# Four-layer graph network on one core: layer 0's attention queries, table building and a long convolution cut into steps and placed elsewhere

## The chip, the core and the metric

The kernel runs on one core of a Trainium2 chip. The core has a matrix engine (TensorE, PE in the profile; its weight loads are shown as PEld), a vector engine (VectorE, DVE), a scalar engine (ScalarE, ACT), a general engine (GpSimd, POOL) and an engine that issues transfers (SyncE, SP). Each takes its instructions in the order of its own queue. The transfers run on 16 DMA engines. The metric is the time on the device in microseconds (us), as the median of the runs; lower is better.

## What is computed

The input is a graph of 1250 nodes with 512 features and 21,250 edges (with 1250 loops in it, and 1250 more for GATv2's mean edges). Four layers follow one another. Each adds a graph network and a linear attention, both of the normalized input, and then a feed-forward part:

```python
xn = _layernorm(x)
x = x + _L0_gnn_ref(xn, ...) + _L0_mix_ref(xn[None], ...)[0]
x = x + _L0_ffn_ref(_layernorm(x)[None], ...)[0]
...                                        # layers 1, 2, 3 alike
```

Three of these twelve parts matter here. The attention of layer 0 and the graph network beside it, which is three GATv2 layers:

```python
# _L0_mix_ref: 8 heads of 64
q, k, v = split(xn @ W_qkv)                # each [1250, 512]
q_phi, k_phi = elu(q) + 1, elu(k) + 1
KV    = einsum('bhnd,bhne->bhde', k_phi, v)
denom = einsum('bhnd,bhd->bhn', q_phi, k_phi.sum(axis=2))[..., None] + 1e-6
out   = einsum('bhnd,bhde->bhne', q_phi, KV) / denom
return out @ W_out + b_out

# _L0_gnn_ref
for k in range(3):
    xl, xr = x @ Wl[k] + bl[k], x @ Wr[k] + br[k]
    m     = leaky_relu(xl[src2] + xr[dst2] + ea2 @ We[k])
    alpha = segment_softmax(m @ att[k], dst2)
    out   = segment_sum(xl[src2] * alpha[:, None], dst2) + b_out[k]
    x     = relu(layernorm(out + x) * gamma[k] + beta[k])
```

The graph network of layer 2 (EGC), where four aggregated bases are weighted for each of 8 heads:

```python
bases = x @ W_bases                                        # [1250, 4 * 64]
agg   = segment_sum(bases[src] * norm, dst).reshape(n, 4, 64)
w     = (x @ W_comb + b_comb).reshape(n, 8, 4)
out   = einsum('nhb,nbf->nhf', w, agg) + conv_bias + x @ W_res + b_res
return relu(layernorm(out) * gamma + beta)
```

And the feed-forward part of layer 2: a convolution over the nodes (3 taps, gelu, then 3 taps to 10 numbers) gives each node its two experts of ten; a shared convolution (9 taps to 256 channels, silu, then 1 tap) is added:

```python
logits = conv1d(gelu(conv1d(xt, rc_w1) + rc_b1), rc_w2) + rc_b2
vals, idx = top_k(logits, 2);  gates = softmax(vals)
y  = sum over the two experts e of gate * (elu(x @ e_w1[e] + e_b1[e]) @ e_w2[e] + e_b2[e])
sh = conv1d(silu(conv1d(xt, sh_w1) + sh_b1), sh_w2) + sh_b2
return layernorm(x + y + sh) * ln_g + ln_b
```

## The kernel before

The nodes stand in ten tiles of 128 rows (`NT`), the last with 98; x stays in SBUF. A product of a tile with a 512 x 512 matrix (`nat`, L171) is four matmuls, each of which appears in the profile as two passes, so eight rows. `evac` brings results out of PSUM by DVE (L136) and ACT (L134) in turn. `add_to_x` (L185) adds a tile to x on DVE. The order on the engines is that in which the program issues, unless a pool or a dependence holds an instruction back; on SP some stretches have an order written out by hand.

**The start of layer 0, `gat_first`.** The nodes are normalized, turned into `xnT` and stored in memory (`xtab`). For the first GATv2 layer, `gat_tables` builds two tables tile by tile, a left one (513 columns) and a right one, and stores them. Then the linear attention runs, first the keys and values (`P`, `ks`, folded with `W_out` into `kvo`), then the query tiles: for each of the ten tiles a product with `wq` (L171), relu and exp on ACT (L746, L747), five DVE operations (L748, L810, L812, L815, L817), four transposes, a product with `kvo` (L171) and an addition to x. All of this is a generator, of which one step is taken after each one-hot group of the edges (`onehot_steps`, L550 to L573). Then `mean_edges` forms the mean of the edges' features for the loops, by way of tables in memory (the gather L614), and the generator is emptied. When all tiles of this stage are free, the GATv2 layers begin.

**The GATv2 layers, `gatv2_fast` and `gat_layer`.** Edges are worked on in groups of four tiles of 128 (47 groups, 188 tiles). POOL gathers the left rows of a group's edges (`xl`, L231, nine buffers), SP loads the one-hot rows (`nb`, L1251, through ACT's L1267) and the right rows of a block (`hl`, L1244), PE multiplies them (`right`, L1280 and L1281), DVE adds and weights them (L1293, L1296), and later PE mixes them by the attention weights into a block of 107 nodes (`more`, L1347). Four groups make a block. When a block is done, it is normalized, and the tables of the next layer are built from it with the same `gat_tables` (L1166), as late work of the loop. The loop `for i in range(FT + 3)` issues a bit of every kind of work per tile; at its end, a loop empties what is left in the three queues `edge`, `todo` and `late`. The next layer's weights and vectors are prepared during a layer, in steps (`gat_weights`, with a POOL memset L1122 and an addition).

**Layer 2's EGC, `layer2_attn`.** For each of ten tiles: the residual product, the product of the one-hot counts with the bases (L2571, after a cast `cs` of 1280 columns), scalings by the degree (`ag`), and for each of four bases one DVE product of 128 x 512 (`m`, L2585) and one POOL addition (L2588). Beside it the linear attention of layer 2 is issued step by step.

**Layer 2's feed-forward, `layer2_ffn`.** Three forms of the transposed input (L2687, DVE) let a convolution with two neighbouring outputs use fewer products. A piece of the convolution's weights is three loads (L2623) and three POOL operations (L2624 to L2626). `conv` runs the products (L2649) for one half of the channels at a time. The order is: forms; router convolution with gelu (L2701); the shared convolution with silu (L2766), while the routing goes on; the ten second products (L2780, L2782); then the loop over 29 expert tiles (`experts`, L2316 to L2348), which loads the expert's weights (1 MB) and the tokens (`xe`, 256 KB) of a tile up to three tiles ahead.

Of the kernel before, what the change touches and what calls it, by code (L numbers as in the profile page):

```python
# [57 lines left out]
class Net:  # L58
# [675 lines left out]
    def linear_attention_steps(self, xn, xT, w_qkv, w_out, b_out, qscale, finish, added=None,  # L734
                               need=None):
# [14 lines left out]
        with self.tc.tile_pool(name="la", bufs=1) as p, \  # L750
# [6 lines left out]
            ks = p.tile([128, D], F32, name="ks")  # L757
            for half in range(2):
                if half:
                    wq = self.weight(w_qkv[:, 0:D], 4, D)  # L760
                    if qscale != 1.0:
                        nc.gpsimd.tensor_scalar(wq, wq, qscale, None, op0=ALU.mult)
# [23 lines left out]
            kvo = p.tile([128, HT, D], F32, tag="k", name="kvo")  # L786
# [13 lines left out]
            yield  # L800
            Q, QT = {}, {}
# [308 lines left out]
    def gat_weights(self, L, p):  # L1110
# [17 lines left out]
        hl = p.tile([128, 2, D], F32R, tag="tro", name="wehl")  # L1128
# [25 lines left out]
    def gat_tables(self, L, p, t, xT, bank):  # L1154
# [7 lines left out]
        def product(name, c):  # L1162
            def f():
                if c == 0:
                    d[name] = bank()
                nc.tensor.matmul(d[name], lhsT=xT(c), rhs=L[name][:, c, :], start=c == 0,  # L1166
                                 stop=c == 3)
                if c == 3:
                    (left if name == "wl" else right)(d[name])
            return f  # L1170

        def left(m):
            o = p.tile([128, D + 1], F32, tag="tlo", name="tlo")
            nc.scalar.copy(o[:, :D], m)
# [5 lines left out]
        def right(m):  # L1180
            o = p.tile([128, 2, D], F32R, tag="tro", name="tro")
            nc.scalar.copy(o[:, 0, :], m)
# [3 lines left out]
        return [product(name, c) for name in ("wl", "wr") for c in range(4)]  # L1186

    def gatv2_fast(self, L, xtab):
# [5 lines left out]
        with self.tc.tile_pool(name="gat", bufs=2) as p, self.weights(2, 1):  # L1194
            big = p.tile([128, 1], F32, name="big", bufs=1)
            nc.vector.memset(big, 2.0 * BIG)
            self.gat_linear(L, p, p)
            for k in range(3):
                otab = self.dram.tile([NP, D], F32, name="x%d" % (k + 1))
                L = self.gat_layer(L, p, xtab, otab, big)  # L1200
                xtab = otab

    def gat_layer(self, L, p, xtab, otab, big):
# [6 lines left out]
        def prepare():  # L1210
# [6 lines left out]
            if nxt is not None:  # L1217
                nxt.update(self.gat_vectors(k + 1, p))
                steps = self.gat_weights(nxt, p)
# [16 lines left out]
        def load(g):  # L1236
            xl = p.tile([128, GE, W], F32, tag="xl", name="xl", bufs=9)
# [117 lines left out]
        def finish(b):  # L1355
# [44 lines left out]
            def across():  # L1400
# [10 lines left out]
                for t in whole:  # L1411
                    for f in self.gat_tables(nxt, p, t, lambda c, t=t: X[t][:, c, :],
                                             lambda: self.bank("tab", [128, D])):
# [41 lines left out]
        for i in range(FT + 3):  # L1455
# [17 lines left out]
            if i < FT:  # L1473
                right(i)
            if 2 <= i < FT + 2:
# [13 lines left out]
        while edge or todo or late:  # L1489
# [6 lines left out]
            for _ in range(2):  # L1496
                if late:
                    late.popleft()[1]()
        return nxt

    def run(self, fast):
# [4 lines left out]
        with self.tc.tile_pool(name="arm", bufs=1) as self.arm:  # L1506
# [23 lines left out]
            with self.psum():  # L1530
# [36 lines left out]
    def gat_first(self, pv, xtab):  # L1567
        nc, I = self.nc, self.I
        L = self.gat_vectors(0, pv)
        with self.tc.tile_pool(name="l0", bufs=1) as p, \  # L1570
# [3 lines left out]
            with self.tc.tile_pool(name="edge", bufs=1, side="right") as pe, \  # L1574
# [7 lines left out]
                for t in range(NT):  # L1582
# [8 lines left out]
                    lambda o, d: nc.vector.tensor_scalar(o, d, 1e-6, None, op0=ALU.add))  # L1591
                next(attention)

                def steps():
                    for t in range(NT):
                        for i, f in enumerate(self.gat_tables(
# [3 lines left out]
                            if i % 4 == 3:  # L1600
                                yield
                    yield from attention
# [7 lines left out]
                for _ in steps:  # L1610
                    pass
# [699 lines left out]
    def experts(self, table, n, rowI, act):  # L2311
# [5 lines left out]
        with self.tc.tile_pool(name="ex", bufs=2) as p, \  # L2317
                self.tc.manual_schedule(engines={mybir.EngineType.SP}):
            def load(i):
                xe = p.tile([128, D], F32, tag="xe", name="xe", bufs=4)  # L2320
                nc.sync.dma_start(xe, self.rin[i * 128:(i + 1) * 128, :])
                row = nc.sync.value_load(rowI[0:1, i:i + 1], min_val=0, max_val=(n - 1) * 128)
                w = p.tile([128, 2050], F32, tag="w", name="w", bufs=4)
                nc.sync.dma_start(w, table[bass.ds(row, 128), :])
                return xe, w

            ahead = [load(i) for i in range(3)]
            for i in range(ntiles):
                xe, w = ahead.pop(0)
                if i + 3 < ntiles:  # L2330
                    ahead.append(load(i + 3))
# [16 lines left out]
                nc.scalar.dma_start(self.rout[i * 128:(i + 1) * 128, :], o)  # L2348

# [134 lines left out]
    def layer2_attn(self):  # L2484
        nc, I = self.nc, self.I
        added = self.both_added()
        with self.tc.tile_pool(name="l2", bufs=1) as p:
# [17 lines left out]
            with self.tc.tile_pool(name="egc", bufs=2) as tmp, \  # L2505
# [55 lines left out]
                for t in range(NT):  # L2561
# [5 lines left out]
                    self.evac(cs, ct)  # L2567
                    go()
                    y = self.mm([128, parts * 256])
                    for s in range(NT):  # L2570
# [6 lines left out]
                    nc.vector.tensor_scalar(af, y[:, :256], dinv[:, t:t + 1], None,  # L2577
                                            op0=ALU.mult)
# [4 lines left out]
                    for b in range(4):  # L2583
                        m = tmp.tile([128, 8, 64], F32, tag="m", name="m")
                        nc.vector.tensor_tensor(  # L2585
                            m, wt[:, :, b:b + 1].to_broadcast([128, 8, 64]),
                            ag[:, b:b + 1, :].to_broadcast([128, 8, 64]), op=ALU.mult)
# [11 lines left out]

    def layer2_ffn(self):  # L2600
        nc, I = self.nc, self.I
        keep = self.begin_tail("l2t")
        with self.tc.tile_pool(name="l2f", bufs=1) as p, ExitStack() as right:
# [5 lines left out]
            with ExitStack() as es:  # L2609
# [5 lines left out]
                G = {}  # L2615

                def piece(src, f, j):

                    g = cp.tile([128, 4, 4, 128], F32, tag="cw", name="cw", bufs=5)
                    g1 = cp.tile([128, 4, 128], F32, tag="g1", name="g1")  # L2620
                    for i, dst in ((0, g[:, 0]), (2, g[:, 3]), (1, g1)):
                        k = 4 * (3 * j + i)
                        nc.sync.dma_start(dst, src[f][:, k:k + 4, :])  # L2623
                    nc.gpsimd.tensor_tensor(g[:, 1], g[:, 0], g[:, 3], op=ALU.add)  # L2624
                    nc.gpsimd.tensor_tensor(g[:, 2], g[:, 1], g1, op=ALU.subtract)
                    nc.gpsimd.tensor_tensor(g[:, 1], g[:, 1], g1, op=ALU.add)  # L2626
                    G[src.tensor.name, f, j] = g

                rc1, sh1 = I["L2_ffn_rc_w1p"], I["L2_ffn_sh_w1p"]
                order = [(rc1, f, 0) for f in range(4)] + [(sh1, f, j) for f in range(2)  # L2630
# [541 lines left out]
```

## Time and profile before

| | us |
|---|---|
| runs | 4534.72, 4537.75, 4541.73 |
| median | 4537.75 |
| profiled execution | 4585.94 |
| its span, first to last instruction | 4584.0 |

The profiled execution is one of its own, so times read from it are compared with its 4585.94 and not with the median. Where its span goes, by the stages of the program:

| stage | from | to |
|---|---|---|
| layer 0: start, tables, attention, one-hots | 18 | 312 |
| gathers of GATv2 layer 0 | 312.7 | 685.9 |
| gathers of GATv2 layer 1 | 770.9 | 1133.3 |
| gathers of GATv2 layer 2 | 1214.9 | 1572.4 |
| layer 0's feed-forward | 1622 | 1890 |
| layer 1: attention and graph network; feed-forward | 1890; 2880 | 2880; 3101 |
| layer 2: EGC and attention; feed-forward | 3101; 3397 | 3397; 3811 |
| layer 3: attention and graph network; feed-forward | 3811; 4226 | 4226; 4584 |

Between the gathers of two GATv2 layers lie some 80 to 85 us in which the last blocks of the one are finished, the last tables built, and the first groups of the next one fetched.

A row of the timeline or of the groups of instructions gives the line, the engine, the operation, out<-in, the shapes and how often it ran; what stands behind the bar or in square brackets is the idle time of the engine just before, and what ended it. A row of the busy time by stretch gives the stretch, its length, and for each engine its busy time and number of instructions; then the clock that PE was granted as a share of the full one, the mean share of the DMA engines in use, and GB/s.

### The profile page before, as it was taken

The numbers are of one execution on the slowest core, as the hardware profiler recorded it, in microseconds if no ns is written. First come the engines' busy times: TensorE is split into PE (matmuls) and PEld (weight loads), VectorE is DVE, ScalarE is ACT, GpSimd is POOL, SyncE is SP. The second block draws the span as 40 slices with busy tenths as digits, with TensorE's granted clock in tenths as the row PEclk, the third lists the DMA queues.
The fourth block names the chain that finished last, engine by engine and source line by source line (L and its number), as shares of the span: only waits on it lengthen the run. The fifth ranks groups of instructions, "written<-read, shape, count | busy, mean of one in ns | idle before, by whom it ended". The sixth has DMA issues, their size and how long they took to land. (4 is left out here: it accounts for less than half of the span.)

```text
span 4584.0 us, 49281 instructions
## 1 busy us (share of the span) xinstructions
PE 3946.8 (86%) x15451; PEld 2434.6 (53%) x15466; DVE 2706.4 (59%) x6387; ACT 1502.9 (33%) x2738; POOL 1402.3 (31%) x1339
## 2 busy tenths in 40 slices
PE   6988998899788866799999999997969975898796
PEld 3435554555354444444788876564546552454474
DVE  5358784878398865533796767314692136587301
ACT  2213332334133354110364446122221122455121
POOL 2027662766366501102000000103253003676101
PEclk9989998999899978899999999999989997997798
DMA  6446664666466423401421110392012185565695
GB/s 221 150 123 199 184 188 138 192 185 187 130 180 189 145 66 105 121 18 59 147 68 42 44 41 21 140 336 80 12 54 71 69 282 154 162 205 170 244 338 188
DMA packets 283000, 647.57 MB, mean 141 GB/s; under 512 B 61673, under 2 KB 108905, under 8 KB 267322
## 3 DMA queue, kind: packets, MB, share of 16 engines
q1 hardware_dynamic: 169290, 357.13, 23.5%
q0 software_dynamic: 73088, 234.75, 17.9%
q10 hardware_dynamic: 40352, 52.44, 3.4%
q8 instruction: 127, 2.08, 0.2%
q14 instruction: 143, 1.17, 0.1%
HBM read 528.87 MB, written 120.65 MB: 142 GB/s over the span
## 5 line engine op out<-in xcount | busy, mean ns | idle before, releaser
L231 POOL DMA_INDIRECT xl<-xl,srcI x564 | 606.6, 1075 | 309.4 <-issue 137.4
L1347 PE MATMUL more<-xl,wT 128*128 128x512 f32 x1128 | 578.5, 600 | 26.8 <-ACT wT L1337 25.3
L1280 PE MATMUL mm<-hl,oh 121*128 121x512 f32 x564 | 419.6, 744 | 89.7 <-DVE s L1293 29.7
L1293 DVE TENSOR_TENSOR s<-xl,mm 128x512 f32<-128x512 f32 x534 | 355.0, 680 | 99.9 <-PE mm L1281 42.3
L1296 DVE SCALAR_TENSOR_TENSOR junk<-s,att 128x512 f32<-128x512 f32 x534 | 409.8, 767 | 6.2
L2099 PE MATMUL more<-hh,e 128*128 128x259 f32 x1600 | 384.0, 386 | 11.1 <-ACT o L2042 8.9
L2099 PEld LDWEIGHTS more<-hh,e 128*128 128x128 f32 x1600 | 295.0, 191 | 75.6 <-issue 16.0
L171 PE MATMUL mm<-w,xnT 128*128 128x512 f32 x640 | 307.7, 620 | 13.7 <-DVE xnT L136 5.3
L231 POOL DMA_INDIRECT g<-routed_out,getI x60 | 64.7, 1079 | 676.7 <-DMA routed_out<-o 490.0
L231 POOL DMA_INDIRECT hs<-gcn_h,srcI x188 | 215.5, 1146 | 96.5 <-issue 35.9
L1347 PEld LDWEIGHTS more<-xl,wT 128*128 128x128 f32 x1128 | 196.5, 192 | 86.2 <-ACT wT L1337 34.4
L1281 PE MATMUL mm<-hl,oh 121*128 121x512 f32 x564 | 238.2, 422 | 0.0
L1280 PEld LDWEIGHTS mm<-hl,oh 121*128 121x128 f32 x564 | 111.6, 198 | 232.6 <-issue 135.0
L2649 PE MATMUL mm<-form,cw 128*128 128x312 f32 (+1 forms) x640 | 181.2, 445 | 23.9 <-POOL cw L2626 10.5
L171 PEld LDWEIGHTS mm<-w,xnT 128*128 128x128 f32 x640 | 123.8, 198 | 141.6 <-issue 125.2
L2019 ACT ACTIVATE e<-r,hh 128x512 f32<-128x512 f32 (+1 forms) x240 | 154.2, 646 | 132.5 <-PE more L2099 121.5
L1267 ACT ACTIVATE oh<-nb 112x512 fp32r<-112x512 bf16 x141 | 88.5, 629 | 327.4 <-DMA nb<-nbt 232.9
L2925 PE MATMUL more<-hl,oh 128*128 128x512 f32 x376 | 166.3, 545 | 31.0 <-ACT hl L2885 11.2
L1166 PE MATMUL tab<-w,xT 128*128 128x512 f32 x320 | 165.1, 614 | 19.9 <-DVE junk L1176 18.1
L2022 ACT ACTIVATE e<-r,a 128x512 f32<-128x512 f32 (+1 forms) x240 | 152.3, 646 | 69.4 <-DVE e L2024 57.2
L2024 DVE TENSOR_TENSOR e<-e,e 128x512 f32<-128x512 f32 (+1 forms) x240 | 142.0, 598 | 51.5 <-ACT e L2019 45.1
L1281 PEld LDWEIGHTS mm<-hl,oh 121*128 121x128 f32 x564 | 113.1, 201 | 106.9 <-issue 105.4
(623 smaller groups left out, 7748.6 us busy)
## 6 DMA issues: line engine op xcount, KB each, us to landing
w<-L_ffn_Wp SPq DMA_DIRECT2D x64, 1024.0 KB
w<-L_ffn_table SPq DMA_DIRECT2D x56, 1025.0 KB
neg<-ntab SPq DMA_DIRECT2D x80, 320.0 KB
nb<-nbt SPq DMA_DIRECT2D x141, 128.0 KB
hl<-xr SPq DMA_DIRECT2D x36, 448.0 KB
xr<-tro SPq DMA_DIRECT2D x30, 512.0 KB
xe<-routed_in SPq DMA_DIRECT2D x56, 256.0 KB
routed_out<-o ACTq DMA_DIRECT2D x56, 256.0 KB
```

Source lines behind the costliest of these rows:

```text
L171: self.nc.tensor.matmul(p, lhsT=xT[:, c, t * 128:(t + 1) * 128], rhs=w[:, c, n0:n0 + n], start=c == 0, stop=c == k - 1)
L231: self.nc.gpsimd.indirect_dma_start(out=out, out_offset=None, in_=table, in_offset=bass.IndirectOffsetOnAxis(ap=idx, axis=0), bounds_check ...
L1166: nc.tensor.matmul(d[name], lhsT=xT(c), rhs=L[name][:, c, :], start=c == 0, stop=c == 3)
L1280: nc.tensor.matmul(m, lhsT=s, rhs=hl[:K, 0, :], start=True, stop=False)
L1281: nc.tensor.matmul(m, lhsT=s, rhs=hl[:K, 1, :], start=False, stop=not on_pe(i))
L1293: nc.vector.tensor_tensor(o, d["xl"][:, j, :D], s, op=ALU.add)
L1296: nc.vector.scalar_tensor_tensor(junk, s, 0.0, L["att"], op0=ALU.max, op1=ALU.mult, accum_out=d["lg"][:, j:j + 1])
L1347: nc.tensor.matmul(B[b]["y"], lhsT=d["wT"][:, j, :], rhs=d["xl"][:, j, :D], start=k == 0 and j == 0, stop=last and j == GE - 1)
L2019: nc.scalar.activation(e1[:, :n], R[q, k, 0][:, :n], AF.Exp, bias=HH[q][:, s, 256:257])
L2099: nc.tensor.matmul(ys[j], lhsT=e[:, j * 128:(j + 1) * 128], rhs=HH[q][:, s, :], start=s == 0, stop=s == NT - 1)
L2649: nc.tensor.matmul(m, lhsT=g[:, which, c, :], rhs=forms[form][:, c, q % 2, q // 2:q // 2 + n], start=j + c == 0, stop=j + 1 == len(gs) and ...
L2925: nc.tensor.matmul(y, lhsT=oh, rhs=hl[:, i], start=i + j == 0 and not (self.fast and k), stop=last and i + j == GE)
```

## The change

Five things are changed.

1. Layer 0's queries. The attention in `gat_first` ends with `kvo`; the bias is added to x at once, and `wq`, `ks` and `kvo` are kept in the pool of the GATv2 layers. A new function gives the six steps of a query tile: fetch the tile's normalized input from memory, turn it, product with relu and exp, division, turn, product and addition to x. Tiles 0 to 2 are handed to GATv2 layer 0, 3 to 6 to layer 1, 7 to 9 to layer 2. In a layer, one step is taken in each of the first 24 turns of its loop, behind `right`; in the loop that empties a layer's queues, one step of the next layer's queries is taken per turn, as long as more than twelve are left.
2. `gat_tables` gives ten steps for a tile instead of eight: the copy to SBUF stays with the last product, the rest is a step of its own. Its store tiles have one buffer in the GATv2 layers instead of two; the `xl` buffers are eight instead of nine.
3. EGC: the cast of the counts and the first scaling go to ACT always; of the four weighted products two stay on DVE, and two become eight ACT operations of 128 x 64 each.
4. Layer 2's feed-forward: the pieces of convolution weights come from a pool of three (five before), of which the first is begun before the stage; the transposed input is brought out by ACT alone; the addition of `ln_b` to x moves from the forms behind the second products. The shared convolution becomes a generator that runs beside the experts: ten steps ahead of the loop and two in each turn, but for turns 7 to 9; from turn 23 on, once it is used up, the second products of a tile stand in its place.
5. `experts` loads weights and tokens by separate functions, weights first; layer 2 has three buffers for each instead of four.

```diff
 def query_steps(self, p, x0, t):        # new
+    def turned(src):
+        q = self.tp([128, 4, 128])
+        for c in range(4):
+            nc.tensor.transpose(q[:, c, :], src[:, c * 128:(c + 1) * 128], self.ident)
+        o = p.tile([128, 4, 128], F32, tag="xT", name="qT", bufs=3)
+        nc.scalar.copy(o, q)
+        return o
...
+    def fetch():
+        d["x"] = flat("qx")
+        nc.sync.dma_start(d["x"], x0[t * 128:(t + 1) * 128, :])
+    def turn():
+        d["xT"] = turned(d["x"])
+    def query():
+        m = product(d["xT"], wq)
+        r = flat("qr")
+        nc.scalar.activation(r, m, AF.Relu, scale=-1.0)
+        nc.scalar.activation(r, r, AF.Exp, scale=-1.0)
+        q = d["q"] = p.tile([128, D], F32, tag="h", name="q")
+        nc.vector.scalar_tensor_tensor(q, m, 0.0, r, op0=ALU.max, op1=ALU.add)
+    def divide():
...
+    def back():
+        d["qT"] = turned(d["q"])
+    def add():
+        self.add_to_x(t, product(d["qT"], kvo))
+    return [fetch, turn, query, divide, back, add]

 def gatv2_fast(self, L, xtab):
+    queries = [deque(f for t in ts for f in self.query_steps(p, x0, t))
+               for ts in ((0, 1, 2), (3, 4, 5, 6), (7, 8, 9))]

 def gat_layer(self, L, p, xtab, otab, big, queries):
-            xl = p.tile([128, GE, W], F32, tag="xl", name="xl", bufs=9)
+            xl = p.tile([128, GE, W], F32, tag="xl", name="xl", bufs=8)
...
             if i < FT:
                 right(i)
+            if queries[k] and i < 24:
+                queries[k].popleft()()
...
         while edge or todo or late:
...
+            if nxt is not None and len(queries[k + 1]) > 12:
+                queries[k + 1].popleft()()

 def layer2_attn(self):
-                    self.evac(cs, ct)
+                    nc.scalar.copy(cs, ct)
...
-                        nc.vector.tensor_tensor(
-                            m, wt[:, :, b:b + 1].to_broadcast([128, 8, 64]),
-                            ag[:, b:b + 1, :].to_broadcast([128, 8, 64]), op=ALU.mult)
+                        if b < 2:
+                            nc.vector.tensor_tensor(
+                                m, wt[:, :, b:b + 1].to_broadcast([128, 8, 64]),
+                                ag[:, b:b + 1, :].to_broadcast([128, 8, 64]), op=ALU.mult)
+                        else:
+                            for h in range(8):
+                                nc.scalar.activation(m[:, h, :], ag[:, b, :], AF.Copy,
+                                                     scale=wt[:, h, b:b + 1])

 def layer2_ffn(self):
-                        self.transpose_tile(xp[:, :, 4 + t * 128:4 + (t + 1) * 128], z[:, t, :])
+                        q = self.tp([128, 4, 128])
...
+                        nc.scalar.copy(xp[:, :, 4 + t * 128:4 + (t + 1) * 128], q)
...
-                        nc.gpsimd.tensor_tensor(self.x[:r, t, :], self.x[:r, t, :], be[:r],
-                                                op=ALU.add)
...
+                def beside(i):
+                    for _ in range(10 if i < 0 else 0 if 7 <= i < 10 else 2):
+                        if next(steps, self) is self and left and i >= 23:
+                            second(left.pop(0))
...
-                self.experts(I["L2_ffn_table"], 10, rowI, elu)
+                self.experts(I["L2_ffn_table"], 10, rowI, elu, 3, beside)
```

## What was predicted

> **What bounds the kernel now.** First the share of the engines and the forty slices: TensorE (PE) is busy for 86% of the span, and no other engine passes 60%, so a change has to shorten the stretches where PE works without pause, or fill those where it waits.
>
> ```profile
> PE 3946.8 (86%) x15451; PEld 2434.6 (53%) x15466; DVE 2706.4 (59%) x6387; ACT 1502.9 (33%) x2738; POOL 1402.3 (31%) x1339
> ...
> PE   6988998899788866799999999997969975898796
> ```
>
> Next the busy time by stretch, because the change touches five places with different limits. Columns: stretch, its length, busy time of PE, PE's weight loads, DVE, ACT, POOL with counts, granted PE clock, DMA share, GB/s.
>
> ```profile
> 227.50:312.70 85.20, 80.15 (x265) 38.71 (x263) 48.71 (x98) 20.34 (x36) 1.00 (x2) 0.96 0.20 57
> 312.70:375.00 62.30, 36.23 (x103) 21.27 (x104) 33.35 (x85) 8.43 (x17) 46.80 (x49) 0.70 0.84 246
> 375.00:700.00 325.00, 299.56 (x1087) 172.07 (x1087) 271.58 (x712) 127.48 (x235) 215.66 (x221) 0.99 0.65 188
> 700.00:770.90 70.90, 61.54 (x174) 29.24 (x172) 23.53 (x61) 19.20 (x37) 7.59 (x7) 0.95 0.30 97
> 770.90:830.00 59.10, 38.11 (x99) 20.72 (x100) 29.68 (x80) 7.49 (x15) 40.38 (x44) 0.68 0.69 208
> ...
> 1199.00:1285.00 86.00, 54.21 (x151) 28.18 (x150) 40.24 (x108) 12.01 (x23) 44.52 (x50) 0.82 0.52 155
> ...
> 3245.00:3397.00 152.00, 129.32 (x365) 67.77 (x363) 136.28 (x262) 47.54 (x76) 60.32 (x40) 0.94 0.06 19
> ...
> 3511.00:3654.00 143.00, 138.90 (x482) 87.51 (x482) 28.35 (x95) 11.49 (x20) 23.36 (x23) 0.98 0.21 78
> 3654.00:3811.00 157.00, 125.05 (x681) 88.90 (x679) 53.75 (x144) 45.51 (x144) 0.00 (x0) 0.96 0.76 256
> ```
>
> The end of layer 0's attention (first row) is PE alone: 80 of 85 us. The steady GATv2 layer (third row) is PE at 92% with DVE at 84%. The beginnings of the three GATv2 layers (second, fifth, sixth row) leave PE idle for 26.1 + 21.0 + 31.8 = 79 us. The end of a layer (fourth row) leaves it 9.4. The shared convolution of layer 2 (row before the last) is PE's, while the expert loop (last row) waits for transfers, as the groups of that stretch say: four transposes open a tile, and most of PE's idle time lies ahead of them.
>
> ```profile
> L160 PE MATMUL tp<-ident,xe 128*128 128x128 f32 x106 | 18.3, 293 | 27.7 <-DMA xe<-routed_in 27.6
> ```
>
> Then single rows of the timeline: the first gather of the GATv2 layers, and the forms of layer 2's convolution.
>
> ```profile
> 312.66 1.03 POOL L231 DMA_INDIRECT xl<-xl,srcI  x1 [42.83 <-DVE big L1196]
> ```
>
> ```profile
> 3404.70 7.31 DVE L2687 TENSOR_TENSOR form<-xp 128x512 f32<-128x512 f32 x12
> 3404.79 8.34 POOL L2625 TENSOR_TENSOR cw<-cw,g 128x512 f32<-128x512 f32 x1
> ...
> 3426.17 10.07 DVE L2687 TENSOR_TENSOR form<-xp 128x512 f32<-128x512 f32 x6
> ...
> 3433.98 13.15 POOL L2690 TENSOR_TENSOR x<-x,be 128x512 f32<-128x512 f32 x10
> ...
> 3447.17 1.11 ACT L2701 ACTIVATE rc<-y,cv 128x313 f32<-128x313 f32 x2 [9.10 <-POOL x L2690]
> ```
>
> The first gather starts when the last tile of layer 0's attention is added. DVE and POOL slow each other: twelve form operations take 7.31 us (0.61 each) while one POOL operation stretches to 8.34, and six take 10.07 (1.68 each) while POOL runs its own at full pace.
>
> **Part A, queries moved out of layer 0's end.** Before, from 227.5 the last seven one-hot groups, the chain of mean edges and ten query tiles share the time. The last one-hot result is copied at 253.0; the chain behind it (a store, a load, a store, the gather at 268.87, two transposed blocks, eight stores ending at 278.8) is 26 us of landings. With the queries gone, a group is some 1.6 us (0.69 DVE, four transposes at 0.22, four products at 0.17), so seven end near 239, the chain at 265: the first gather comes 312.7 - 265 = 48 us sooner. That is the gain. It can be 38 (groups waiting on their stores) to 56.
>
> What comes back: a tile is 16 product passes at the issue pitch of 0.43 in this stretch = 6.9, plus eight transposes (four of the fetched x are new) at 0.15 = 1.2: 8.1 us of PE, 81 for ten; with it 3.8 us DVE (0.69 four times, 0.68 for the add, three small), 2.4 us ACT, and a 256 KB fetch on SP. In the changed program's order three tiles stand in the first 24 steps of layer 0, two whole tiles and the first product of another ahead of the last blocks' work at the end of layer 0, one tile and one product at the end of layer 1, the rest in the next beginnings. At the ends PE has no room (9.4 of 70.9 idle): I take 16 us of 16 to 20 for the first and 8 of 8 to 12 for the second. In the beginnings 49 us meet 79 us of idle time; bounds 0 (all hidden) and 49 (each step stands ahead of the next `right` product in PE's queue and delays it). I take 9, nearer to hidden, since the idle time is larger at each of them.
>
> In the beginning of layer 0 the queues also get longer. The two weight loads of the next layer (2 MB), issued at 278.95 under the queries before, now fall into a stretch that moves 246 GB/s at a share of 0.84: 8 us of transfer, of which 6 fall on the path. SP's load of the edge rows waits there behind a POOL memset, which now stands behind 26 gathers, not 22, at a pitch of 1.3: 5 us; behind it in SP's queue wait the one-hot loads of the next groups, and for them ACT and PE. Gather buffers fall from nine to eight: POOL already waits 64.8 us in all for L1347 to free them; bounds 0 and 8, taken 3. Tables in ten steps and single store buffers: nothing, since the store of one tile lands some 20 us before the next copy; 2 us a tile otherwise.
>
> Sum of A: -48 + 16 + 8 + 9 + 6 + 5 + 3 = -1 us; bounds about -30 and +30.
>
> The Trainium skill, "TensorE: Matmul & The Clock Gate", Part 1, says that an array idle for a few microseconds falls to half clock until it has been busy as long. The rows agree in kind: 0.96 where the queries stood, 0.70 and 0.68 in two beginnings. By it the 49 us could cost up to 70% more there, or raise the clock for all that stands beside them.
>
> **Part B, layer 2's EGC attention.** DVE is busy 136 of 152 us and PE 129. DVE loses 20 of the 40 weighted products (L2585, 1.06 us beside POOL), ten scalings (0.48) and eight casts (0.80): 32 us. ACT takes 160 small 128x64 activations. No row has one; bounds are 0.20 (128x1) and 0.30 (128x128, L2791); at 0.25, 40 us, with copies of 1.36 and scalings of 0.47 some 55 us on top of 48. So ACT reaches 103 of 152, and PE becomes the limit. It is idle 22.7 us there, some 7 of them at the first and last tile, which stay: at most -15. POOL's adds will wait for eight activations instead of one product, which can cost 5. I take -6, bounds -15 and +5.
>
> The Trainium skill, "ScalarE: Activation LUTs", What ACT_TABLE_LOAD costs, gives an activation with a pointer operand as 280 ns plus 0.833 ns an element, overlapping its neighbour by 93. It would make of each some 240 ns, an estimate from that page, and of all 38 us instead of 40.
>
> **Part C, forms and router convolution.** Of the POOL work between 3400 and 3447 only three pieces (nine operations) remain; the ten bias adds (L2690, 13.15 us) go behind the experts, and the transposed copies go to ACT (ten at 0.58). The twelve contended forms fall from 1.56 to 1.68 to 0.61: 12 x 1.0 = 12 us of DVE; the wait of 9.1 for the gelu goes. On the path: PE idles 21 of 50 us there (its clock 0.73). I take -12, bounds -16 and -4 (if the pieces, three ahead instead of five, come late).
>
> **Part D, shared convolution beside the experts.** Before: convolution 3511 to 3620, second products to 3650, experts to 3811 (29 tiles, 5.4 us each). After: 62 of 192 products come before the first expert tile, so the loop starts near 3556, not 3654. A product is two passes of 0.275 (L2649's start-to-start in the timeline), 0.55; an expert tile alone is 4.4 us of PE (125.05 over 28 of them). Tiles 0 to 6 with the 34 products left of the first half: 7 x 4.4 + 34 x 0.55 = 49; 7 to 9: 14; tile 10 waits for three pieces whose loads come late on SP behind POOL's sums (a single spare buffer): 18; 11 to 21 with eight products each, 8.75: 96; 22: 5; 23 to 27 with two second products each (3.0, from 30 us for ten): 51; 28: 7. That is 240, end at 3796 instead of 3811: -14; bounds -28 (no stall, DMA as before) and +5 (three buffers in place of four and the convolution's 3 MB in a transfer-bound loop). I take -14. Layer 1's experts issue weights before tokens; DMA bounds them either way: 0.
>
> **Sum.** -1 - 6 - 12 - 14 = -33 us against the profiled execution of 4586 (span 4584.0 and 1.9 around it): 4553. That execution lies 48 us, 1.06%, above the median of 4537.75; scaled by it, 4505.
>
> **Rivals.** (1) The ends hide the queries as well: PE stood waiting for DVE or ACT between blocks, and A is -38. For it: PE's records are modelled ends, so busy is not full; against: 61.5 busy of 70.9. Total -70, 4468. (2) The moved queries cost more than they gave: PE takes its queue in order, each step holds the `right` products behind it, all 81 us are paid and the start's 14 us too: A = -48 + 95 = +47, total +15, 4553. For it: PE and DVE are both near full in the layers; against: 79 us idle. It decides from A above +32 on. (3) The transfers rule layer 2 anyway: the expert loop stays bound by DMA, C gives 4 and D nothing. Total -11, 4527. That the change does nothing of the kind is ruled out for A by the order of the instructions.
>
> **From this to the numbers.** Forecast 0.55, rival 1 0.18, rival 2 0.13, rival 3 0.14. The forecast's own range is 4480 to 4530; the predicted time is 4505. With A's bounds (30 either way), B 10, C 6, D 16 taken as independent, about 35 us; reaching to the rivals, 4458 to 4546. A measurement of this kernel tells about 0.2%, 9 us, from no change: faster is below 4528.7, same up to 4546.8. Faster: 0.50 + 0.18 + 0.10 = 0.78; same 0.04 + 0.04 + 0.03 = 0.11; slower 0.11.
>
> **What would show it.** The first gather near 265; layer 0 to 1's gap (711 to 771 before) longer by 16; in the EGC stretch DVE below 115 and ACT near 100; no POOL row L2690 before the gelu; a first expert tile near 3556 less the earlier gains, and a PE pause at the tenth. It would be wrong if the GATv2 layers lengthen by over 60 us, or if the expert loop lasts past 250.

## The result

| six runs each | median, us | lowest | highest |
|---|---|---|---|
| before | 4542.19 | 4534.72 | 4552.93 |
| changed | 4570.80 | 4566.90 | 4585.70 |

The changed kernel is slower: its time is 1.0065 times that of before, 95% interval [1.0046, 1.0085], some 30 us. A drop of 33 us was forecast. A second set of runs gave 1.0078 [1.0048, 1.0107].

Since the kernel before took 4588.59 us (median) beside the first four experiments, 4542 to 4549 beside all others, and 4585.94 in its profiled execution, the two profiled spans are not subtracted here, ratios are always against runs of before in the same group, and differences of two profiles are read as rough. 1% is taken as 45 us.

The shares of the engines in the changed kernel, and its busy time by stretch with the columns as before:

```profile
PE 3924.5 (86%) x15491; PEld 2428.0 (53%) x15506; DVE 2713.3 (59%) x6342; ACT 1589.2 (35%) x2949; POOL 1393.0 (30%) x1339
```

```profile
264.70:327.00 62.30, 36.69 (x104) 19.83 (x105) 29.05 (x71) 7.66 (x13) 41.62 (x44) 0.78 0.86 267
352.00:689.50 337.50, 306.50 (x1084) 175.42 (x1082) 279.84 (x685) 124.21 (x233) 214.99 (x220) 0.96 0.61 179
689.50:782.00 92.50, 82.81 (x245) 39.82 (x243) 38.00 (x86) 29.38 (x51) 9.79 (x8) 0.96 0.30 92
...
1231.30:1317.30 86.00, 75.56 (x246) 40.39 (x245) 58.51 (x152) 21.44 (x42) 46.54 (x52) 0.96 0.58 178
3268.00:3420.00 152.00, 130.32 (x377) 66.55 (x375) 117.15 (x233) 97.62 (x249) 56.44 (x40) 0.97 0.05 15
...
3568.00:3813.00 245.00, 220.56 (x1011) 146.84 (x1009) 69.88 (x171) 71.78 (x168) 23.72 (x19) 0.98 0.59 193
```

Layer 2 went near the forecast: in the EGC stretch DVE fell from 136 to 117 us (the forecast was below 115) and ACT rose from 48 to 98; the expert loop with the convolution beside it lasts 245 us. Layer 0's end is short as forecast too:

```profile
264.70 1.03 POOL L231 DMA_INDIRECT xl<-xl,srcI  x1 [12.81 <-DVE big L1278]
```

The first gather comes at 264.7, 48 us sooner. But the next layer's first gather, 770.9 before, comes at 782.0: layer 0 alone lasts 59 us longer, and layer 1 another 21. The loss is in the GATv2 layers, and the prediction's own sign of being wrong, that they lengthen by over 60 us, has come.

### The profile page after: what moved, and what is told of

The parts are those of the page before. It is cut to its first block, busy times and chain, and to the rows that moved or that the text cites. A ratio compares the mean times of both kernels' runs of the same rounds, so it can differ in the third digit from the quotient of the medians.

```text
span 4570.3 us, 49685 instructions
## 1 busy us (share of the span) xinstructions
PE 3924.5 (86%) x15491; PEld 2428.0 (53%) x15506; DVE 2713.3 (59%) x6342; ACT 1589.2 (35%) x2949; POOL 1393.0 (30%) x1339
## 3 DMA queue, kind: packets, MB, share of 16 engines
q8 instruction: 127, 2.08, 0.2%
## 5 line engine op out<-in xcount | busy, mean ns | idle before, releaser
L1432 PE MATMUL more<-xl,wT 128*128 128x512 f32 x1128 | 590.9, 611 | 52.1 <-ACT wT L1422 51.6
L1381 DVE SCALAR_TENSOR_TENSOR junk<-s,att 128x512 f32<-128x512 f32 x534 | 433.0, 811 | 6.8
L171 PE MATMUL mm<-w,xnT 128*128 128x512 f32 x560 | 267.5, 616 | 15.1 <-DVE xnT L136 5.4
L3082 PE MATMUL more<-hl,oh 128*128 128x512 f32 x376 | 163.5, 538 | 22.8 <-DVE oh L3046 9.8
L171 PEld LDWEIGHTS mm<-w,xnT 128*128 128x128 f32 x560 | 108.0, 197 | 125.4 <-issue 108.5
L160 PE MATMUL tp<-ident,xn 128*128 128x128 f32 x280 | 50.1, 324 | 131.9 <-DVE rsx L207 41.5
L2056 PE MATMUL mm<-w,xnT 128*128 128x258 f32 x640 | 158.8, 392 | 5.0 <-DVE junk L2040 4.6
```

The costliest lines, as they stand in the source:

```text
L171: self.nc.tensor.matmul(p, lhsT=xT[:, c, t * 128:(t + 1) * 128], rhs=w[:, c, n0:n0 + n], start=c == 0, stop=c == k - 1)
L1381: nc.vector.scalar_tensor_tensor(junk, s, 0.0, L["att"], op0=ALU.max, op1=ALU.mult, accum_out=d["lg"][:, j:j + 1])
L1432: nc.tensor.matmul(B[b]["y"], lhsT=d["wT"][:, j, :], rhs=d["xl"][:, j, :D], start=k == 0 and j == 0, stop=last and j == GE - 1)
L2056: nc.tensor.matmul(m, lhsT=chunk(layer, c)[:, t * 128:(t + 1) * 128], rhs=w[:, c, :], start=c == 0, stop=c == k - 1)
L3082: nc.tensor.matmul(y, lhsT=oh, rhs=hl[:, i], start=i + j == 0 and not (self.fast and k), stop=last and i + j == GE)
```

## The experiments

Two theories stood after this. Theory Q: the moved queries cost all their TensorE time. Theory T: the tables' steps and the fewer buffers cost part of it, since stretches of layers 0 and 1 in which no query runs were longer too.

**1 and 2. Part A undone; queries left out.** The first has the changed kernel's other parts with the queries in layer 0's end, tables in eight steps, two store buffers, nine gather buffers. The second is the changed kernel without these lines:

```diff
-            if queries[k] and i < 24:
-                queries[k].popleft()()
...
-            if nxt is not None and len(queries[k + 1]) > 12:
-                queries[k + 1].popleft()()
```

> The changed kernel with part A undone: the queries are back in layer 0's end, the tables take eight steps with two store buffers, nine gather buffers; parts B, C, D stay. If all of the loss lies in part A, as the stages of the two profiles say (layer 2's EGC 5 us shorter, its feed-forward 21 shorter, layer 1's feed-forward 9 longer), this is 17 us below the kernel before, about 4525. By the sum on record (B -6, C -12, D -14) it would be 32 below, about 4510. If parts B to D lose time themselves, it is not below 4540.

> The changed kernel in which the query steps handed to the GATv2 layers are not issued at all (the attention's result is left out of x). Theory Q: the ten query tiles alone make the layers longer (81 us of PE work, none of it hidden); then without them the layers last as long as before and the 48 us of the earlier start remain: about 4542 - 48 - 17 = 4477. Theory T: part of the loss is in the ten table steps, the single store buffers and the eight gather buffers, since groups 24 to 32 and 40 to 46 of layers 0 and 1 are 8 to 11 us longer each although no query runs there; some 37 us then stay and this is about 4514.

Measured: 0.9936 [0.9910, 0.9961], -29 us, and 0.9892 [0.9873, 0.9912], -49 us. Parts B to D give nearly what the record's sum said (-32), so the error is in part A. Between the changed kernel (1.0065 and 1.0078) and the second lie 1.7 to 1.9%, some 80 us (ratios of different groups of runs): as much as the whole TensorE time of the queries (81). Yet without queries and with the start 48 us sooner it gains just 20 us over the first: some 25 are lost to the tables or the buffers. Both theories hold in part.

**3, 4, 7, 9, 10. Steps and buffers apart**, all on the kernel before and without moved queries:

```diff
-            xl = p.tile([128, GE, W], F32, tag="xl", name="xl", bufs=9)
+            xl = p.tile([128, GE, W], F32, tag="xl", name="xl", bufs=8)
...
-                                             lambda: self.bank("tab", [128, D])):
+                                             lambda: self.bank("tab", [128, D]), 1):
```

> The kernel before with only the ten table steps, one store buffer instead of two, and eight gather buffers instead of nine; no query is moved. Theory T: 37 us longer, about 4579, in layers 0 and 1 and not in layer 2. Theory Q: within 9 us of the kernel before.

> The kernel before with eight gather buffers instead of nine. If the buffers are what makes the layers of theory T longer (POOL's queue stands at a gather and holds back the additions of the normalization and the softmax behind it), 20 to 40 us longer, in all three layers. By the sum on record 3 us. Theory Q: 0.

> The kernel before with the tables in ten steps instead of eight, but two store buffers and nine gather buffers as before. The three edits together cost 39 us and eight gather buffers 21, so 18 are left for the ten steps and the single store buffer. Theory 'steps': a tile has ten pieces in the queue of late work, of which every second turn takes one, so more is left for the layer's end: 10 to 18 us longer. Theory 'store buffer': within 5 us of the kernel before.

> The kernel before with the tables in ten steps and one store buffer instead of two, nine gather buffers. Against the same with two store buffers (0.59% below the kernel before) it tells the store buffer's price. If prices add (the three edits 39 us, ten steps -27, eight gather buffers 21), one store buffer costs 45 us and this is 18 us above the kernel before. If the price of e3 comes only from both shortages together, this stays below the kernel before.

> The kernel before with ten steps, two store buffers and eight gather buffers. If prices add: -27 + 21, some 6 us below the kernel before. If eight buffers hurt only where DVE stands still for the tables, it keeps most of the 27.

| steps | store buffers | gather buffers | ratio to before | interval |
|---|---|---|---|---|
| 8 | 2 | 8 | 1.0047 | [1.0029, 1.0065] |
| 10 | 2 | 9 | 0.9941 | [0.9916, 0.9965] |
| 10 | 1 | 9 | 0.9943 | [0.9926, 0.9960] |
| 10 | 2 | 8 | 1.0064 | [1.0041, 1.0087] |
| 10 | 1 | 8 | 1.0085 | [1.0067, 1.0103] |

Ten steps, expected to cost 10 to 18 us, gain 27. The single store buffer costs nothing with nine gather buffers, and with eight the two intervals overlap; the 45 us put on it before the ninth run were wrong, because prices don't add. The loss comes with the step from nine gather buffers to eight: 21 us with eight steps, 56 with ten (1.0064 against 0.9941).

Why the steps gain is read from the waits of DVE and TensorE, between 375 and 1140 us (engine, instruction and tile, released by: us in total, times, longest). Before, then ten steps:

```profile
DVE junk L1176 <- ACT tlo L1174: 72.9, 16, 9.1
...
PE tab L1166 <- DVE junk L1176: 15.2, 14, 1.4
```

```profile
DVE junk L1182 <- ACT tlo L1171: 26.1, 4, 8.0
...
PE tab L1166 <- DVE junk L1182: 1.4, 1, 1.4
```

With eight steps the weighting of a table stood in DVE's queue right behind the product, and DVE waited for TensorE's product and ACT's copy; as a step of its own it comes a turn or more later, and DVE does other work. TensorE's wait for the weighting, before its next product for a table, falls from 15.2 us to 1.4. How the 27 us divide among the waits was not tested.

Why eight buffers lose shows in the same view, ten steps with nine and then with eight buffers:

```profile
ACT h L1403 <- POOL h L1400: 51.3, 19, 6.8
...
POOL lin L1267 <- DVE lg L1308: 45.7, 25, 8.1
...
PE more L1353 <- ACT wT L1343: 5.5, 6, 1.4
```

```profile
ACT h L1403 <- POOL h L1400: 148.3, 18, 17.7
...
POOL lin L1267 <- DMA xl<-xl,srcI: 58.6, 17, 4.9
...
PE more L1353 <- ACT wT L1343: 52.6, 17, 10.6
```

and in the timeline with eight buffers, in layer 0:

```profile
571.55 1.04 POOL L231 DMA_INDIRECT xl<-xl,srcI  x1 [0.30 <-issue]
...
572.56 0.81 ACT L1394 ACTIVATE h<-h,rs 107x512 f32<-107x512 f32 x1
...
576.05 0.19 POOL L1267 TENSOR_TENSOR lin<-xl,ae 128x4 f32<-128x4 f32 x1 [3.46 <-DVE junk L1302]
576.76 1.36 POOL L231 DMA_INDIRECT xl<-xl,srcI  x1 [0.51 <-issue]
...
582.07 1.28 POOL L1451 TENSOR_TENSOR c<-c,b_out 107x512 f32<-107x512 f32 x1
...
583.30 1.26 POOL L1399 TENSOR_TENSOR h<-h,gamma 107x512 f32<-107x512 f32 x1
584.64 1.60 POOL L1400 TENSOR_TENSOR h<-h,beta 107x512 f32<-107x512 f32 x1
...
586.28 0.63 ACT L1403 ACTIVATE h<-h 107x512 f32<-107x512 f32 x1 [10.65 <-POOL h L1400]
587.72 0.59 ACT L1343 COPY wT<-tp 128x512 f32<-128x512 f32 x1 [0.81 <-ACT h L1403]
588.36 1.22 PE L1353 MATMUL more<-xl,wT 128*128 128x512 f32 x1 [4.87 <-ACT wT L1343]
```

ACT has scaled the block's `h` by 573.4, but in POOL's queue a `lin`, four gathers and the addition of a bias (`c`) stand ahead of the multiplication, and it runs at 583.3. ACT waits 10.65 us for the result in its own order, behind that wait stands the copy of the next mix's weights (`wT`), and TensorE waits for the copy. The mix is what frees a gather buffer, and the next gathers in turn stand behind the normalization in POOL's queue. With nine buffers the same `lin` and the four gathers behind it are over at 562.2, before the scaling at 562.87 to 563.7, and ACT waits 0.73 us at the same block (the sixth):

```profile
555.55 0.20 POOL L1267 TENSOR_TENSOR lin<-xl,ae 128x4 f32<-128x4 f32 x1 [1.67 <-DVE lg L1308]
...
566.76 0.63 ACT L1403 ACTIVATE h<-h 107x512 f32<-107x512 f32 x1 [0.73 <-POOL h L1400]
```

What makes `lin` late is its place in the queue. This one is of the 31st group, and with eight buffers 31 x 4 = 124 gathers stand ahead of it: it comes right behind the gathers of its own group, whose rows it needs. With nine, 128 gathers are ahead of it, and another group's gathers lie between. Where the trace has the landing, a `lin` with eight buffers starts 0.2 us behind the last of its own gathers (566.78 after 566.56, 605.59 after 605.38). Counted over the traces of layers 0, 1 and 2, a `lin` stands directly behind its own gathers 19, 22 and 4 times of 47 with eight buffers and ten steps, 9, 12 and 4 times with eight buffers and eight steps, and once a layer with nine. POOL's idle time before `lin` in layers 0 and 1 is 141 us, 105 us and, with nine, 47 (ten steps) or 55 (before). The prices stand in the same order, 56 us, 21 us and none. That the eighth and ninth buffer make the price is shown by the runs; the chain behind it is read from the traces, and no run moved `lin` or the normalization alone.

Another measure that suggests itself does not give the price: how long a buffer is held, from a group's first gather to the end of its eighth mix pass, divided by the pace of the loop. In layer 0 that is 70.5 us (median of 47 groups) at 8.0 us a group (24 groups in 191.9), 8.8 groups, with ten steps and nine buffers, and 71.7 us at 8.5 (24 in 204.2), 8.4 groups, before. But with eight buffers and ten steps it is 65.2 us at 9.3, 7.0 groups, and with ten buffers (experiment 15) 76.6 us at 7.9, 9.7 groups. It grows with the number of buffers that there are; by 9.7 groups nine would be short, and they are as fast as ten.

**6, 5, 8, 11. What the queries give and cost.** The kernel before without query tiles; the changed kernel again; its queries spread over the layers; its queries without relu, exp and division:

```diff
-            if queries[k] and i < 24:
+            if queries[k] and i >= 28 and (i - 28) % 40 < 6:
...
-            if nxt is not None and len(queries[k + 1]) > 12:
-                queries[k + 1].popleft()()
```

> The kernel before in which the ten query tiles of layer 0's attention are left out altogether (the attention's result is missing from x; keys, values, bias and all else stay). Theory: the first gather comes 48 us sooner, near 265, and the whole 48 us stay to the end, 1.05% less. Rival: the beginnings of the layers are held by transfers and give part of it back, so that less than 35 us remain.

> The changed kernel itself, unaltered, on the same chip as the next three, as their yardstick: 0.65% above the kernel before, some 30 us. If its distance to the kernel without query steps is the whole work of the queries, its GATv2 layers take some 75 us longer than that kernel's.

> The changed kernel with the query tiles neither at the beginnings nor at the ends: the six steps of a tile are taken in turns 28 to 33, 68 to 73, 108 to 113 and 148 to 153 of a layer. Theory 'crowding': the loss comes from placing them where the chain to the first mix and the layer's end is short of nothing but time, so this is 20 to 40 us faster than the changed kernel. Theory 'no room': TensorE sets the pace of the layers everywhere, 8 us a tile wherever it stands, so this is within 9 us of the changed kernel.

> The changed kernel in which a query tile keeps its fetch, its eight transposes, its sixteen product passes and the addition to x, but loses relu, exp and the five DVE operations of the division (3.1 us of DVE and 0.6 of ACT a tile; the attention's result is then not the reference's). Theory 'PE': the 70 us that the queries cost in the layers are TensorE's, so this is within 10 us of the changed kernel (0.65 to 0.78% above the kernel before). Theory 'DVE': VectorE, 84% busy, is as much the limit, so 25 us or more are saved.

Measured: 0.9903 [0.9875, 0.9932], -44 us, so most of the earlier start is kept to the end. The changed kernel: 1.0078; from the first gather of layer 0 to the last of layer 2 its profile takes 57 us more than that of the second experiment, not the 75 expected. Spread: 1.0047 [1.0028, 1.0065], 8 to 14 us better than the changed kernel, below the 20 to 40 of 'crowding' and at the edge of 'no room'. Without the division: 1.0041 [1.0026, 1.0057], 11 to 17 us better, between the two theories (within 10, or 25 and more), so of 80 us some 65 belong to what was kept; that TensorE's work is most of it is likely but not shown.

**13, 14. Queries with nine gather buffers**, with and without the query steps. To make room, the second product uses the query weights in place of the folded matrix, so these two leave out the folded matrix and show times alone:

```diff
-                self.queries = wq, ks, kvo
+                self.queries = wq, ks, wq
```

> The changed kernel with nine gather buffers instead of eight. To make room, the folded matrix of the attention isn't kept, and the second product of a query tile uses the query weights in its place (the same work, another result). Theory 'shortage': eight buffers are what makes the changed kernel slow, and with nine the moved queries are worth their place: 56 us faster than the changed kernel or more, at or below the 0.9865 of parts B, C, D with ten steps. Theory 'no room': nine buffers give the 56 us back, the queries still cost some 70 for the 44 of the earlier start, so this is near 0.992, above 0.9865.

> The same with the query steps left out. Its distance to the run before is the price of the queries with nine buffers. Theory 'no room': 65 to 80 us, as with eight, so 0.976 to 0.978. Theory 'shortage': 30 us or less of price, since a late mix then doesn't hold the gathers.

Measured: 0.9896 [0.9879, 0.9912] and 0.9797 [0.9776, 0.9818]. The ninth buffer is worth 1.7 to 1.8%, some 80 us, to the changed kernel. The queries' price falls from 80 to 45 us, between the two theories, and equals the 44 of the start. (The two profiled executions lie 61 us apart, more than the runs' medians; in them the three beginnings and two ends add 58.) By stretch, without query steps and then with them (beginning of layer 0 up to group 8, steady part, end, beginning of layer 1):

```profile
265.50:344.50 79.00, 48.69 (x151) 29.77 (x151) 44.13 (x118) 11.30 (x23) 53.68 (x58) 0.74 0.77 242
344.50:648.10 303.60, 291.31 (x1055) 167.74 (x1053) 272.31 (x689) 125.51 (x233) 210.98 (x214) 0.99 0.68 194
648.10:715.50 67.40, 57.73 (x162) 27.42 (x160) 22.32 (x50) 17.72 (x34) 6.98 (x6) 0.95 0.34 105
715.50:773.20 57.70, 43.87 (x144) 25.07 (x145) 39.82 (x108) 11.09 (x21) 46.11 (x52) 0.85 0.78 230
```

```profile
264.60:366.40 101.80, 72.38 (x223) 40.12 (x223) 58.65 (x147) 18.38 (x35) 54.44 (x60) 0.84 0.64 199
366.40:667.50 301.10, 289.01 (x1053) 166.93 (x1052) 271.75 (x681) 125.67 (x233) 209.71 (x212) 0.99 0.67 194
667.50:744.60 77.10, 74.07 (x222) 35.53 (x220) 29.48 (x64) 26.97 (x47) 7.51 (x5) 1.00 0.32 100
744.60:813.80 69.20, 55.42 (x181) 30.91 (x181) 47.22 (x122) 13.02 (x27) 48.91 (x53) 0.90 0.69 203
```

In the first row TensorE works 23.7 us more and the stretch is 22.8 longer: its idle time, 30.3 against 29.4, is hardly used. In layer 1 both grow by 11.5. Only the end of layer 0 hides some: 16.3 more work in 9.7 more time. In the same places eight buffers change little (100.8 and 68.0 us in the changed kernel), but its steady part lasts 334 us instead of 301, though no query runs in it: there the shortage takes its price.

**12, 15. A version that beats both.** Parts B, C, D and ten steps, queries left in layer 0's end, nine gather and two store buffers; then one store buffer and ten gather buffers.

> Parts B, C and D together with the ten table steps, with the queries left in layer 0's end, two store buffers and nine gather buffers. -29 and -27 touch different stages, so they should add: 1.2% below the kernel before. If the layers' gain is only in some executions, less than 0.9%.

> Parts B, C, D and ten table steps, queries in layer 0's end, with one store buffer instead of two (which cost nothing) and the room given to a tenth gather buffer. If the layers still wait for gather buffers (32 us of POOL's idle time stood before a release with nine), 5 to 20 us below 0.9865; if nine are enough, the same.

Measured: 0.9865 [0.9841, 0.9889], some 61 us less than before (56 by the sum of its parts), and 0.9879 [0.9862, 0.9895], the same within the intervals: nine buffers are enough. The first is the best version found; the queries in the layers with nine buffers, 0.9896, don't improve on it.

## Why the prediction was wrong

**Right.** The first gather at 265 (264.7), kept to the end (44 of 48 us). Parts B, C, D: -32 forecast, -29 measured. By the profiles, with seven of the old forms against ten of the new: from EGC's first weighted product to the first form 149.6 to 151.7 us against 145.6 to 145.7 (-4 to -6; -6 forecast); from the first form to the first gelu 47.3 to 48.0 against 31.6 to 32.3 (some -16; -12); from there to the last expert tile 346 to 349 against 331 to 339 (-8 to -18; -14). Layer 1's experts, where 0 was forecast, go the other way: from the first to the last tile 110 to 115 us with tokens loaded first, 115 to 125 with weights first, some 6 us more in the mean. That was not tried apart.

In single terms: 160 small activations at 0.25 us, 40 us,

```profile
L2694 ACT ACTIVATE m<-ag,comb 128x64 f32<-128x64 f32 x160 | 39.9, 334 | 24.7 <-POOL out L2696 24.7
```

39.9 busy, 249 ns each, as their 334 ns overlap. By the Trainium skill's 280 ns plus 0.833 an element less 93 ("ScalarE: Activation LUTs", What ACT_TABLE_LOAD costs) it would be some 240 ns each, an estimate from that page. DVE's own relief in EGC was smaller than said, 19 us and not 32.

The forms are a gain by luck in part. The twelve contended ones were to fall to 0.61 us each:

```profile
3422.77 25.98 DVE L2817 TENSOR_TENSOR form<-xp 128x512 f32<-128x512 f32 x27 [0.16 <-ACT xp L2810]
```

Of the 30 forms nine still take 1.74 to 1.76 us beside the nine POOL operations that are left, where eleven did before; the others take 0.68 to 0.70. The gain is that 27 run without a pause, and that the gelu no longer waits 9.1 us for the bias additions. The expert loop was put at 240 us and lasts 245; tiles 13 to 21 start 8.2 us apart (8.75 was taken), and the pause for the late pieces is there, 24 us between two tiles instead of 18.

**Wrong, and decisive: "Gather buffers fall from nine to eight: ... bounds 0 and 8, taken 3."** Measured 21 us with eight steps, 56 with ten, some 80 with the queries. The step took its price from how long POOL had waited for buffers, 64.8 us, which says nothing of the queue with one buffer less. It named nothing behind the gathers in POOL's queue. There, with eight buffers, stands the `lin` of the same group, which waits for them to land (POOL's idle time before `lin` 141 us instead of 47); behind it stands the normalization, behind that ACT's copies, and behind these the mix that frees buffers.

**Wrong: "49 us meet 79 us of idle time; ... I take 9, nearer to hidden".** In three beginnings the queries cost 40 us even with nine buffers (22.8 + 11.5 + 6.0, the last from 64.5 us in layer 2 against 58.5). TensorE's three longest pauses at the beginning of layer 0 are 9.3, 7.0 and 7.6 us without queries and 9.2, 6.8 and 5.1 with them: the queries do not fill them, and the third is then a wait for a query's own input, whose fetch SP issued only at 304.9:

```profile
309.43 1.09 PE L1219 MATMUL tp<-ident,qx 128*128 128x128 f32 x4 [5.06 <-DMA qx<-x]
```

That the rest is paid because each query step delays the next `right` is argued from the order of TensorE's queue, not shown apart. At the ends 24 us were taken and 17 paid (9.7 and 7.6); there the program issues two tiles and one, without the further products that the prediction names.

**Wrong, the other way: "Tables in ten steps ... : nothing".** They gain 27 us with nine buffers; DVE's waits of 72.9 us for `tlo` stood in the trace of before and weren't used.

**The sum of A** was -1. With nine buffers it would have been near: -44 - 27 + 45 = -26 (0.9896 against 0.9936 says -18). The missing ninth buffer turned it into +58 to +64 (1.0065 and 1.0078 against 0.9936). Rival 2 (4553 us) had the sign, but its mechanism, all 81 us paid because each step holds the products behind it, is at most half of what was found: with nine buffers 45 are paid; the other half is the shortage, which no rival named.

With queries the granted clock in the beginning of layer 2 rose from 0.82 to 0.96, and with nine buffers in that of layer 0 from 0.74 to 0.84. This agrees in kind with the Trainium skill ("TensorE: Matmul & The Clock Gate", Part 1), by which an array idle for some microseconds falls to half clock until it has been busy as long. It bought little: layer 0's beginning still grew by nearly all of the queries' work, 22.8 of 23.7 us. The 70% that the prediction names beside that page was not worked out there and follows from no row here.

## What to carry to other kernels

Before a buffer is taken away, ask what then stands right behind the fill in its engine's queue. Here it was an instruction that reads the same fill, and it held back everything behind it, up to the work that frees the buffer. Neither the waits for buffers summed before the edit nor the time that a buffer is held tells the price; a run with one buffer less, beside the other edits, does. Idle time of an engine at the beginning of a pipelined loop can be waiting for inputs, not room for other work; work moved there was paid almost in full. Prices of edits that share a resource don't add; the pair has to be run.

## What the runs showed of the hardware

A wait of TensorE costs more than its own length. In the run with ten steps and eight buffers, after the wait of 4.87 us that ends at 588.36, the granted clock is 0.51 for three microseconds (columns as before), and a pair of mix passes takes 2.08 us; from 591.72 on it takes 1.02 again, as it did ahead of the wait:

```profile
588.00:591.00 3.00, 2.64 (x4) 1.41 (x5) 0.00 (x0) 0.84 (x2) 2.38 (x3) 0.51 0.75 207
```

By the trace's clock records it falls to half in this way four times in layer 0 between 415 and 700 us with eight buffers, and never there with nine.

DVE slows beside POOL: in the changed kernel a 128x512 form takes 0.68 us with POOL idle, and nine of the eleven that ran beside POOL's operations on the weights took 1.74 to 1.76 us.
